# One increment per run of matmuls: no-dependency groups with a fence in a graph layer with quantile aggregation

## The chip, the cores and the metric

The kernel runs on one core of one Trainium2 chip. The metric is the device time of one execution in microseconds (us). Before the change three runs gave 2081.84, 2082.70 and 2082.77 us, so the median is 2082.7 us.

A core has five engines with a queue of instructions each: PE (TensorE, matrix products, results go to PSUM), DVE (VectorE), ACT (ScalarE), POOL (GpSimd) and SP (SyncE, here it only issues DMAs). Each works through its queue in order. They wait for each other through semaphores: an instruction can add to its engine's semaphore when it is done, and an instruction of another engine can wait until that semaphore has reached a value.

## The reference

There are 16 graphs of 1024 nodes with 64 channels each. What is computed, cut to what matters:

```python
h = max(layernorm(x), 0)
neigh = (adj > 0) & ~eye
rank = cumsum(neigh) - neigh                      # place of a neighbour in its row
nb = neigh.sum(-1)
skip = where(nb > 10, (nb + 1) // 2, 1)
rem = neigh & (skip > 1) & (rank % skip == skip - 1) & mask
rem = rem | rem.T                                 # edges that are dropped
nd = where(rem, 0, adj with ones on the diagonal) > 0
s = sort of h over the nodes of nd, for each node and channel
agg = 0.25 * q(0.25) + 0.5 * q(0.5) + 0.25 * q(0.75)   # interpolated quantiles of s
out = h + agg
y = relu(out @ W1 + b1) @ W2 + b2
return x + y * mask
```

A graph row has about eight neighbours, so the kernel keeps lists of neighbours and not matrices of values.

## The kernel before

The kernel has two ways through: `list_layer`, which runs, and `dense_layer`, a loop for inputs whose rows have too many neighbours, which the program skips here. All that follows is `list_layer`.

For each graph `b` these steps are made, as Python generators whose yields hand over to the next one:

- `load`: SP reads eight adjacency tiles of 128 x 1024 (L570), two ahead. ACT makes signs of a tile (L646), PE transposes it with eight matmuls against an identity into two PSUM tiles "tp" (L652; L657 takes the diagonal away), ACT or DVE copies them as fp8 into "ne" (L660, L662).
- `number`: 16 matmuls (L682) and eight (L689) count neighbours; six short DVE instructions (L693 to L699) follow.
- `drop`: for each half tile five matmuls (L712, L717) give the place of every neighbour in "rk", ACT takes a distance (L721), and DVE compares (L722) into "rem".
- `keep`: for each half tile six matmuls (L733, L734, L737) take dropped edges away in "kp", ACT copies (L738), then eight matmuls (L741) code the kept edges into "code", and ACT copies into "pack" (L744).
- `order`: DVE counts (L750 on), 16 matmuls (L764, L766, L770) give each node its place by number of neighbours, and DVE writes the permutation (L779).
- `collect`: for each of eight tiles nine matmuls (L801, L805) permute "pack" into "codeP", ACT copies three parts out (L809, L813, L814), and DVE draws neighbour numbers out of the codes (L819 to L848) into the list "idx". L848 is the last instruction of a list.
- `normalize`: the layer norm, on ACT (L894 to L913), and two tables of rows in DRAM.

For each pair `m` of graphs, these steps follow:

- `fetch` puts 134 gathers into a Python queue. `issue` takes them out: each is an indirect DMA on POOL (L965) and behind it a small `iota` on POOL (L942). Every fourth gather is made to wait for a DVE instruction of 12 noted instructions ago, which paces the gathers.
- `aggregate`: `sort` runs a network of minima and maxima on DVE over the gathered rows (L1000, L1003, L1007) with small pauses (L982), multiplies them by weights (L1014), and PE sums each group of rows into "acc" (L1016, L1053). `terms` splits the sum (L1028, L1030).
- `mlp`: DVE writes a 0/1 matrix "at_p" (L1077), PE brings the sums back to the order of the nodes with eight matmuls into "high" (L1096) and eight into "low" (L1099), ACT copies both (L1104, L1106), PE multiplies by W1 (L1109, L1110), ACT does the relu (L1112), and `output` multiplies by W2 (L1122, L1126) and adds x on DVE (L1129, L1130).
- Nodes with many neighbours are put together over eight graphs: `fetch_group` (L1148, L1152), `aggregate_group` and `scatter` (L1191).

PSUM has eight buffers: three of tag "mx" (tp, cp, rk, kp), one "misc" (mp, nb, ps, hp, yp and others), two "code" (code, codeP), two "agg" (acc, high, low, gacc).

`weave` mixes the results of one pair with the preparation of the graphs after the next one by costs that the generators yield. This sets the order in which instructions are written. The order in which an engine's queue holds them is made afterwards by the scheduler of the recording layer, which knows the dependencies of instructions through the tiles that they read and write and a model of times. The layer then writes the semaphores: which instruction adds to its engine's semaphore, and who waits for which value. A matmul of 7858 that `list_layer` makes stands in the queue behind a load of its weights, except where the product is of fp32.

The functions that the diff touches, and what calls them:

Of the kernel before, what the change touches and what calls it, by code (L numbers as in the profile page):

```python
# [41 lines left out]
P = 128  # L42
# [3 lines left out]
NT = N // P  # L46
# [493 lines left out]
def list_layer(  # L540
# [20 lines left out]
    psum = ctx.enter_context(tc.tile_pool(name="psum", bufs=1, space=bass.MemoryType.PSUM))  # L561
    dram = ctx.enter_context(tc.tile_pool(name="dram", bufs=2, space=bass.MemoryType.DRAM))

    asked = {}

    def ask(b, t):
# [70 lines left out]
    def load(b, fast=False):  # L637

        ne = wk.tile([P, NT, N], FP8, name="ne", bufs=2)
        neT[b] = ne  # L640
        nbs[b] = [wk.tile([P, NT], F32, name=n) for n in ("bias", "half")]
        for t in range(NT):
            ask(b, t)
            at = asked.pop((b, t))
            sg = wk.tile([P, N], BF16, name="sg")
            nc.scalar.activation(sg, at, AF.Sign)  # L646
            ask(*divmod(b * NT + t + 2, NT))
            for n in range(2):
                tp = psum.tile([P, 4, P], F32, name="tp", tag="mx", bufs=3)
                for s in range(4):  # L650
                    m = 4 * n + s
                    nc.tensor.matmul(  # L652
                        tp[:, s], sg[:, m * P:(m + 1) * P], ident16, start=(s == 0), stop=(s == 3 and t // 4 != n),
                        skip_group_check=True,
                    )
                if t // 4 == n:
                    nc.tensor.matmul(tp[:, t % 4], minus16, ident16, start=False, stop=True, skip_group_check=True)  # L657
                to = ne[:, 4 * n:4 * n + 4, t * P:(t + 1) * P]
                if fast:
                    nc.vector.tensor_scalar(to, tp, 0.0, None, OP.max, saturate=False)  # L660
                else:
                    nc.scalar.activation(to, tp, AF.Relu, saturate=False)  # L662
            if fast and t == 3:
                number(b, 0, 4)
            yield 0.1
        if fast:
            number(b, 4, NT)
        else:
            number(b, 0, NT)
        yield 1.4  # L670

    def number(b, lo, hi):
# [3 lines left out]
        for n in range(lo // 4, hi // 4):  # L676
            cols = slice(n * HALF, (n + 1) * HALF)

            cp = psum.tile([P, HALF], F32, name="cp", tag="mx", bufs=3)
            for k in range(2):  # L680
                for q in range(4):
                    nc.tensor.matmul(  # L682
                        cp[32 * q:32 * q + 32], one[:, 1 - k:33 - k], ne[:, 2 * q + k, cols], start=(k == 0),
                        stop=(k == 1), skip_group_check=True,
                    )
            nc.scalar.copy(cnt[:, cols], cp)
        nb = psum.tile([P, NT], F32, name="nb", tag="misc")
        for t in range(lo, hi):
            nc.tensor.matmul(nb[:, t:t + 1], cnt[:, t * P:(t + 1) * P], ones16[:, 0:1], start=True, stop=True)  # L689
        nb = nb[:, lo:hi]  # L690

        sk = wk.tile([P, NT], I32, name="sk")[:, lo:hi]
# [8 lines left out]
    def drop(b):  # L701

        ne = neT[b]
        bias, half = nbs[b]
        rem = wk.tile([P, NT, N], BF16, name="rem", tag="wide", bufs=1)
        rems[b] = rem
        for t in range(NT):
            ts = slice(t * P, (t + 1) * P)
            dist = wk.tile([P, N], F16, name="dist")
            for n in range(2):  # L710
                rk = psum.tile([P, HALF], F32, name="rk", tag="mx", bufs=3)
                nc.tensor.matmul(  # L712
                    rk, cnt[:, ts], blocks[:, 4 * n:4 * n + 4, None].to_broadcast([P, 4, P]), start=True, stop=False,
                    skip_group_check=True,
                )
                for s in range(4):
                    nc.tensor.matmul(  # L717
                        rk[:, s * P:(s + 1) * P], ne[:, 4 * n + s, ts], upper, start=False, stop=(s == 3),
                        skip_group_check=True,
                    )  # L720
                nc.scalar.activation(dist[:, n * HALF:(n + 1) * HALF], rk, AF.Abs, bias=bias[:, t:t + 1])  # L721
            given.append(nc.vector.tensor_scalar(rem[:, t], dist, 1.0, half[:, t:t + 1], OP.add, OP.is_equal))  # L722
            yield 0.5

    def keep(b):

        ne, rem = neT.pop(b), rems.pop(b)
        for t in range(NT):
            ts = slice(t * P, (t + 1) * P)
            kept = wk.tile([P, NT, P], FP8, name="kept")  # L730
            for n in range(2):
                kp = psum.tile([P, 4, P], F32, name="kp", tag="mx", bufs=3)
                nc.tensor.matmul(kp, plus, ne[:, 4 * n:4 * n + 4, ts], start=True, stop=False)  # L733
                nc.tensor.matmul(kp, minus, rem[:, 4 * n:4 * n + 4, ts], start=False, stop=False)  # L734
                for s in range(4):
                    at = (4 * n + s) * P
                    nc.tensor.matmul(kp[:, s], rem[:, t, at:at + P], minus, start=False, stop=(s == 3))  # L737
                nc.scalar.activation(kept[:, 4 * n:4 * n + 4], kp, AF.Relu, saturate=False)  # L738
            code = psum.tile([P, NT, 17], F32, name="code", tag="code", bufs=2)
            for s in range(NT):  # L740
                nc.tensor.matmul(  # L741
                    code[:, s], kept[:, s], octet, start=(s == 0), stop=(s == NT - 1), skip_group_check=True
                )
            nc.scalar.copy(pack[:, t, :KEYS], code.rearrange("p s k -> p (s k)"))  # L744
            yield 0.1

    def order(b):
# [12 lines left out]
        yield 1.5  # L760

        ps = psum.tile(shape, F32, name="ps", tag="misc")
        for t in range(NT):
            nc.tensor.matmul(ps, ones16, more[:, t:t + 1].to_broadcast(shape), start=(t == 0), stop=False)  # L764
        for t in range(NT - 1):
            nc.tensor.matmul(  # L766
                ps[:, t + 1:], ones16, same[:, t:t + 1].to_broadcast([P, NT - 1 - t, CAP]),
                start=False, stop=False,
            )
        nc.tensor.matmul(ps, before16, same, start=False, stop=True)  # L770
        at = wk.tile(shape, F32, name="at_e", bufs=1)
        nc.vector.tensor_tensor(at, ps, same, OP.mult)
        place_f = wk.tile([P, NT], F32, name="place_f")
# [10 lines left out]
    def collect(b, parts=((0, NT),)):  # L784
# [12 lines left out]
        for first, last in parts:  # L797
            for k in range(first, last):
                flat = psum.tile([P, PACKED], F32, name="codeP", tag="code", bufs=2)
                code = flat[:, :KEYS].rearrange("p (s k) -> p s k", k=17)  # L800
                nc.tensor.matmul(  # L801
                    flat[:, :KEYS], ones16, base[:, :KEYS], start=True, stop=False, skip_group_check=True
                )
                for t in range(NT):
                    nc.tensor.matmul(  # L805
                        flat, perm[:, t, k * P:(k + 1) * P], pack[:, t], start=False, stop=(t == NT - 1),
                        skip_group_check=True,
                    )
                nc.scalar.copy(st[:, k], flat[:, OWN:VALUES])  # L809
                halves, bytes_ = (  # L810
                    own[:, k, b % 2].bitcast(d).rearrange("p (c k) -> p c k", c=C) for d in (BF16, U8)
# [173 lines left out]
    def sort(lines, plan, first, coef, acc, in_turn=False):  # L985
# [25 lines left out]
        for n in taken:  # L1011
            now, ends = ends[:n], ends[n:]
            v = at(now[0], now[1] - now[0] if n > 1 else 0, n).rearrange("p s (k c) -> p s k c", c=C)
            nc.vector.tensor_tensor(v, v, coef(first, n)[:, :, :, None].to_broadcast(list(v.shape)), OP.mult)  # L1014
            for s in now:
                nc.tensor.matmul(  # L1016
                    acc, ident32, lines[:, s], start=False, stop=(s == now[-1] and not ends), skip_group_check=True
                )
            first += n
            cost = 0.16 + n * size / 960  # L1020
            held = let_go(held + cost)
# [64 lines left out]
    def mlp(b, o):  # L1086
# [3 lines left out]
        for n in range(2):  # L1090
# [1 line left out]
                yield from one_hot(b, n)  # L1092
            at = placed.pop((b, n))
            high = psum.tile([P, HALF], F32, name="high", tag="agg", bufs=2)
            for t in range(NT):
                nc.tensor.matmul(high, o[:, t, 0:2 * C], at[:, t], start=(t == 0), stop=(t == NT - 1))  # L1096
            low = psum.tile([P, HALF], F32, name="low", tag="agg", bufs=2)
            for t in range(NT):
                nc.tensor.matmul(  # L1099
                    low[C * (t % 2):C * (t % 2) + C], o[:, t, 2 * C:], at[:, t], start=(t < 2), stop=(t >= NT - 2),  # L1100
                    skip_group_check=True,
                )
            highs = wk.tile([P, HALF], F32, name="highs", bufs=1)
            nc.scalar.copy(highs, high)  # L1104
            lows = wk.tile([P, HALF], F32, name="lows", bufs=1)
            nc.scalar.copy(lows, low)  # L1106
            yield 1.0
            hp = psum.tile([P, HALF], F32, name="hp", tag="misc")
            nc.tensor.matmul(hp, w1, highs, start=True, stop=False)  # L1109
            nc.tensor.matmul(hp, w1, lows, start=False, stop=True)  # L1110
            h1 = wk.tile([P, HALF], F32, name="h1", bufs=1)
            nc.scalar.activation(h1, hp, AF.Relu, bias=b1c)  # L1112
            yield 1.0
# [5 lines left out]
    def output(h1, n, mask, x):  # L1119

        yp = psum.tile([P, n, C], F32, name="yp", tag="misc")
        nc.tensor.matmul(  # L1122
            yp, ones_r, b2r[:, None, :].to_broadcast([P, n, C]), start=True, stop=False, skip_group_check=True
        )
        for k in range(n):
            nc.tensor.matmul(  # L1126
                yp[:, k], h1[:, k * P:(k + 1) * P], w2, start=False, stop=(k == n - 1), skip_group_check=True
            )
        nc.vector.tensor_tensor(yp, yp, mask[:, :, None].to_broadcast([P, n, C]), OP.mult)  # L1129
        nc.vector.tensor_tensor(x, x, yp, OP.add)  # L1130

# [327 lines left out]
```

## Time and profile before

The profile is of one execution. Its span, from the first to the last instruction, is 2466.9 us; the page gives no other time of that execution. The timed runs, with a median of 2082.7 us, are of executions without a profile.

| | before |
|---|---|
| timed runs, us | 2081.84, 2082.70, 2082.77 |
| span of the profiled execution, us | 2466.9 |
| mean granted TensorE clock | 0.710 |
| gathers L965 | 1072, 1102.8 us busy, 1029 ns mean |
| sort step L1003 | 408, 280.6 us busy, 704 ns mean |
| transposing matmul L652 | 1024, 116.2 us busy, 260 ns mean |
| codeP matmul L805 | 1024, 198.3 us busy, 340 ns mean |
| sum matmul L1016 | 448 records, 160.3 us busy, 514 ns mean |
| moved by DMA | 130.22 MB, mean 53 GB/s |

How to read what the profile has: "busy" is the time in which an engine had an instruction of a row under way. A row of the waits reads: engine and line that waited, the line that released it, then the microseconds in total, how many times, and the longest. A row of the timeline reads: start, length, engine, line, operation, tiles, count, and in square brackets the idle time of the engine before it and what ended it. "issue" means that nothing the profile shows was waited for. "PEld" is the load of weights.

### The profile page before, as it was taken

To read this page: it belongs to the slowest core of one execution; us is meant where nothing else is said; L and a number is where in the kernel's file an instruction comes from. 1 tells how busy PE (TensorE), PEld (TensorE's weight loads), DVE (VectorE), ACT (ScalarE), POOL (GpSimd) and SP (SyncE) were. 2 spreads that over 40 slices of the span, in tenths; PEclk is the share of its full clock that TensorE was granted. 3 is DMA by queue.
4 is the path that set the end of the run, shared out by engine and by line. 5 is a ranking of instruction groups with operands and counts; after the bars stand their busy time and mean duration, and the time that the engine had idled before them with its cause. 6 is when DMAs were issued, how large, how long until landed. Compare 5 with 4: busy or idle time off the path is not lost.

```text
span 2466.9 us, 26583 instructions
## 1 busy us (share of the span) xinstructions
PE 1195.3 (48%) x8366; PEld 725.7 (29%) x8385; DVE 1173.0 (48%) x3635; ACT 926.8 (38%) x2414; POOL 1430.4 (58%) x2201
## 2 busy tenths in 40 slices
PE   6327165435484438345385546535565455430216
PEld 4114033222242224223153324323333233210113
DVE  3303168221356444354257452858447354931883
ACT  7428255334463236234274445433534232100001
POOL 0750846464758674676748674756577666888000
PEclk9658577667686768666686777767676777665658
DMA  3322222121313131221223131310312100111000
GB/s 109 97 64 75 62 57 73 35 60 43 91 46 77 31 89 46 48 62 41 67 71 91 42 79 29 90 46 16 93 40 60 32 17 16 42 23 20 17 0 12
DMA packets 152602, 130.22 MB, mean 53 GB/s; under 512 B 117570, under 2 KB 118082, under 8 KB 152450
## 3 DMA queue, kind: packets, MB, share of 16 engines
q1 hardware_dynamic: 116482, 91.51, 13.2%
q0 software_dynamic: 35968, 36.90, 8.4%
q8 instruction: 68, 1.11, 0.2%
q14 instruction: 84, 0.69, 0.1%
HBM read 112.78 MB, written 13.81 MB: 51 GB/s over the span
## 4 chain that ended last, share of the span: by engine, by line
PE 28%; another core or an unknown queue 22%; DVE 14%; POOL 12%; ACT 11%; issue 11%; DMA 2%; SPq 0%; POOLq 0%; DVEq 0%; ACTq 0%
POOL g L965 8%; PE codeP L805 3%; PE kp L737 3%; PE acc L1016 3%; ACT dist L721 3%; DVE g L1003 3%; DVE g L1007 2%; POOL spent L942 2%; PE kp L734 2%; PE kp L733 2%; ACT sg L646 2%; PE tp L652 2%; ACT kept L738 2%; PE rk L712 2%
## 5 line engine op out<-in xcount | busy, mean ns | idle before, releaser
L965 POOL DMA_INDIRECT g<-htab,idx x1072 | 1102.8, 1029 | 790.6 <-issue 237.6
L1003 DVE TENSOR_TENSOR g<-g 128x768 f32<-128x768 f32 (+3 forms) x408 | 280.6, 704 | 223.0 <-DMA g<-htab,idx 200.6
L942 POOL IOTA spent<- 128x128 int16 x1072 | 267.3, 249 | 44.6 <-remote 1.5
L1007 DVE TENSOR_TENSOR g<-g 128x512 f32<-128x512 f32 (+3 forms) x408 | 278.9, 702 | 22.9 <-PE acc L1053 8.4
L1016 PE MATMUL acc<-g,kf 128*128 128x256 f32 (+2 forms) x448 | 160.3, 514 | 186.2 <-DVE g L1014 160.5
L652 PE MATMUL tp<-kb,sg 128*128 128x128 bf16 x1024 | 116.2, 260 | 271.0 <-ACT sg L646 119.0
L721 ACT ACTIVATE dist<-rk,bias 128x512 f16<-128x512 f32 x256 | 172.0, 696 | 186.8 <-remote 90.2
L738 ACT ACTIVATE kept<-kp 128x512 fp8e4<-128x512 f32 x256 | 150.5, 600 | 192.0 <-remote 130.4
L662 ACT ACTIVATE ne<-tp 128x512 fp8e4<-128x512 f32 x240 | 137.3, 605 | 193.5 <-remote 136.1
L805 PE MATMUL codeP<-pack,perm 128*128 128x332 bf16 x1024 | 198.3, 340 | 9.2 <-DVE pause L982 5.5
L652 PEld LDWEIGHTS <-sg 128*128 128x128 bf16 x1024 | 88.0, 118 | 296.1 <-issue 144.5
L712 PE MATMUL rk<-kb,cnt 128*128 128x512 bf16 x256 | 118.7, 464 | 109.0 <-ACT dist L721 49.1
L722 DVE TENSOR_SCALAR rem<-dist,half 128x1024 bf16<-128x1024 f16 x128 | 64.0, 502 | 223.3 <-ACT dist L721 181.3
L741 PE MATMUL code<-kw,kept 128*128 128x17 fp8e5 x1024 | 67.8, 176 | 209.5 <-issue 99.6
L1016 PEld LDWEIGHTS acc<-g,kf 128*128 128x128 f32 x448 | 101.9, 268 | 221.9 <-DVE g L1014 170.2
L750 DVE TENSOR_REDUCE num<-pack 128x8 f32<-128x64 bf16 x16 | 4.3, 268 | 303.1 <-ACT pack L744 303.1
L717 PEld LDWEIGHTS <-ne 128*128 128x128 fp8e4 x1024 | 95.0, 114 | 165.7 <-issue 147.0
L646 ACT ACTIVATE sg<-at 128x1024 bf16<-128x1024 f32 x128 | 133.7, 1062 | 14.0 <-DMA at<-in_adj_dram 12.5
L734 PE MATMUL kp<-rem,kw 128*128 128x512 bf16 x256 | 113.8, 445 | 38.6 <-DVE g L1003 38.6
L741 PEld LDWEIGHTS <-kept 128*128 128x128 fp8e4 x1024 | 52.4, 102 | 260.8 <-issue 128.2
L805 PEld LDWEIGHTS <-perm 128*128 128x128 bf16 x1024 | 100.3, 107 | 91.3 <-issue 17.6
L737 PE MATMUL kp<-kw,rem 128*128 128x128 fp8e5 x1024 | 124.0, 244 | 0.0
(157 smaller groups left out, 2297.8 us busy)
## 6 DMA issues: line engine op xcount, KB each, us to landing
at<-in_adj_dram SPq DMA_DIRECT2D x128, 512.0 KB
g<-htab,idx POOLq DMA_INDIRECT x1072
xt<-in_x_dram SPq DMA_DIRECT2D x16, 256.0 KB
htab<-xt SPq DMA_DIRECT2D x16, 256.0 KB
gtab<-xt SPq DMA_DIRECT2D x16, 256.0 KB
y<-in_x_dram SPq DMA_DIRECT2D x16, 256.0 KB
out_dram<-y SPq DMA_DIRECT2D x16, 256.0 KB
gg<-g SPq DMA_DIRECT2D x16, 96.0 KB
```

What stands on the lines that cost most here:

```text
L646: nc.scalar.activation(sg, at, AF.Sign)
L652: nc.tensor.matmul(tp[:, s], sg[:, m * P:(m + 1) * P], ident16, start=(s == 0), stop=(s == 3 and t // 4 != n), skip_group_check=True,)
L712: nc.tensor.matmul(rk, cnt[:, ts], blocks[:, 4 * n:4 * n + 4, None].to_broadcast([P, 4, P]), start=True, stop=False, skip_group_check=True,)
L721: nc.scalar.activation(dist[:, n * HALF:(n + 1) * HALF], rk, AF.Abs, bias=bias[:, t:t + 1])
L737: nc.tensor.matmul(kp[:, s], rem[:, t, at:at + P], minus, start=False, stop=(s == 3))
L738: nc.scalar.activation(kept[:, 4 * n:4 * n + 4], kp, AF.Relu, saturate=False)
L805: nc.tensor.matmul(flat, perm[:, t, k * P:(k + 1) * P], pack[:, t], start=False, stop=(t == NT - 1), skip_group_check=True,)
L942: tc.keep_in_program_order(nc.gpsimd.iota(spent, pattern=[[1, 128]], base=0, channel_multiplier=0))
L965: return nc.gpsimd.indirect_dma_start(out=gathered[m, tiles][:, slot, k - lo, h], out_offset=None, in_=tables[2 * m + h], in_offset=bass.I ...
L1003: given.append(nc.vector.tensor_tensor(at(f, df, n), pa, pb, one))
L1007: nc.vector.tensor_tensor(pa if back else pb, pa, pb, other)
L1016: nc.tensor.matmul(acc, ident32, lines[:, s], start=False, stop=(s == now[-1] and not ends), skip_group_check=True)
```

## The change

A helper `settle` is added. It gets a list of matmuls that fill one PSUM tile, in their order. It ties each to the next by a dependency without a semaphore, puts all but the last in a group in which the layer looks for no dependencies, marks them so that they do not count on PE's semaphore, and names the last as the group's fence. Every place that fills a PSUM tile with more than one matmul collects the instructions and calls it. The matmuls, their operands and flags are the same; so are all other instructions.

```diff
+    runs = [0]
+
+    def settle(run):
+
+        runs[0] += 1
+        for ins, then in zip(run, run[1:]):
+            tc.add_manual_dep(
+                then.ins, ins.ins.name,
+                mybir.DependencyInfo(mybir.DependencyClass.NoSync, mybir.DependencyReason.DATA),
+                reason="order of a run",
+            )
+            tc.add_to_no_dep_group(f"run{runs[0]}", ins.ins)
+            tc.info.no_tile_sem_insts.add(ins.ins.name)
+        if len(run) > 1:
+            tc.declare_fence(run[-1].ins, group=f"run{runs[0]}")
...
                 tp = psum.tile([P, 4, P], F32, name="tp", tag="mx", bufs=3)
+                run = []
                 for s in range(4):
                     m = 4 * n + s
-                    nc.tensor.matmul(
+                    run.append(nc.tensor.matmul(
                         tp[:, s], sg[:, m * P:(m + 1) * P], ident16, start=(s == 0), stop=(s == 3 and t // 4 != n),
                         skip_group_check=True,
+                    ))
+                if t // 4 == n:
+                    run.append(
+                        nc.tensor.matmul(tp[:, t % 4], minus16, ident16, start=False, stop=True, skip_group_check=True)
                     )
-                if t // 4 == n:
-                    nc.tensor.matmul(tp[:, t % 4], minus16, ident16, start=False, stop=True, skip_group_check=True)
+                settle(run)
...
-            for s in now:
+            settle([
                 nc.tensor.matmul(
                     acc, ident32, lines[:, s], start=False, stop=(s == now[-1] and not ends), skip_group_check=True
                 )
+                for s in now
+            ])
...
             high = psum.tile([P, HALF], F32, name="high", tag="agg", bufs=2)
-            for t in range(NT):
+            settle([
                 nc.tensor.matmul(high, o[:, t, 0:2 * C], at[:, t], start=(t == 0), stop=(t == NT - 1))
+                for t in range(NT)
+            ])
```

The same is done to the runs of "cp" (8 matmuls), "nb" (4 or 8), "rk" (5), "kp" (6), "code" (8), "ps" (16), "codeP" (9), "low" (8), "hp" (2) and "yp" (5, or 3 for a group of nodes with many neighbours). In `sort` a run is not the whole of "acc" but the two or more rows that are summed after one multiplication. The single matmuls of "terms" and those that start "acc" are left as they were.

## The prediction

> **What bounds the kernel now.** I read the page from the top: busy shares, chain, waits, then the order of GpSimd's gathers in time.
>
> ```profile
> span 2466.9 us, 26583 instructions
> PE 1195.3 (48%) x8366; PEld 725.7 (29%) x8385; DVE 1173.0 (48%) x3635; ACT 926.8 (38%) x2414; POOL 1430.4 (58%) x2201
> PE 28%; another core or an unknown queue 22%; DVE 14%; POOL 12%; ACT 11%; issue 11%; DMA 2%; SPq 0%; POOLq 0%; DVEq 0%; ACTq 0%
> ```
>
> No engine is full; the chain of work that ended last passes through all of them. So the bound is a relay: PE, ACT and DVE make the neighbour lists, POOL gathers by them, DVE sorts, PE sums. The profiled span is 384 us longer than the median run (2466.9 against 2082.7), and the chain puts 22% down to releasers that it cannot name. I therefore use this profile for durations and differences in microseconds, which I add both to the span and to the median of 2082.7, and not for absolute shares.
>
> The waits, longest first, show the hand-overs:
>
> ```profile
> POOL g L965 <- DVE idx L848: 206.7, 6, 80.5
> DVE g L1003 <- DMA g<-htab,idx: 200.6, 24, 50.0
> POOL g L965 <- DVE pause L982: 159.6, 11, 31.8
> ACT highs L1104 <- PE high L1096: 95.7, 14, 68.2
> PE high L1096 <- DVE at_p L1077: 64.0, 3, 63.3
> ```
>
> POOL waits for the lists (L848), DVE waits for gathered rows, and 11 times POOL's wait for DVE is put down to the pause (L982), a neighbour of the awaited instruction. In POOL's timeline the two largest stalls, 70.89 and 80.53 us, lie before 250 us; after 483 us none is over 32:
>
> ```profile
> 72.78 1.10 POOL L965 DMA_INDIRECT g<-htab,idx  x1 [70.89 <-DVE idx L848]
> 247.10 0.94 POOL L965 DMA_INDIRECT g<-htab,idx  x1 [80.53 <-DVE idx L848]
> 1997.05 1.32 POOL L965 DMA_INDIRECT g<-htab,idx  x1 [11.86 <-DVE bit L844]
> 2041.07 0.95 POOL L965 DMA_INDIRECT g<-htab,idx  x1 [7.62 <-PE acc L1016]
> 2042.32 0.95 POOL L965 DMA_INDIRECT g<-htab,idx  x1 [0.30 <-issue]
> 2043.57 0.94 POOL L965 DMA_INDIRECT g<-htab,idx  x1 [0.30 <-issue]
> ```
>
> Gathers follow each other every 1.25 us (2042.32 to 2043.57), so 1072 of them are a stream of 1340 us that PE cannot shorten. Between 690 and 2270 us I count 20 stalls of POOL over 5 us, together 273 us: what a better or worse order of the other engines can move lies there.
>
> **What the Trainium skill says.** "TensorE: Matmul & The Clock Gate", section "The cost: per-tile semaphore tail": increments that matmuls make on completion serialize, about 26.3 ns each, and one increment on the last suffices because matmuls end in order. No row here shows the 26.3 ns. "Perfetto Trace Analysis", section "Tensor Engine Instruction (MATMUL, LD_WEIGHTS)": the end of a matmul in a profile is estimated, and the semaphore moves later, when PSUM has acknowledged. So a change in that tail would appear as a changed wait of ACT or DVE, not as a shorter matmul; the rows agree at least in that the 128x128 matmul is near one value (L652: 216 minimum, 219 ns median).
>
> **The change, part by part.**
>
> 1. Increments removed. The words of the change suggest 7858 matmuls that now count only at the end of each run. I built both programs and counted, in the part that runs: 1363 of 7858 matmuls carry an increment before, 1287 after. The build before already folds a run's counts into one addition (values of 5, 9 or 13) on the matmul that somebody waits for. Nobody waits for 88 of the 1363 (25 of L1096, 22 of L1016, 22 of L1109, 19 others); after, for 9. So 76 increments go, at 26.3 ns: 2.0 us if all lay on the path, 0.6 us with PE's 28% of the chain. As no row shows the price, I take 1.0 us and keep 0 to 2.0. A larger number in one addition instead of a one could have a price too; the signals that matter are the same ones, and I take nothing.
>
> 2. Waits. Of ACT's 1143 waits on PE before, 1133 name the very same matmul after; of DVE's 269, 261; of POOL's 25, all. No reader is made to wait for a later matmul in numbers that matter. PE's waits on itself go from 495 to 498. Such a wait costs at most the length of the matmul in front, 0.30 us for a codeP matmul (eight in 2.42 us on PE's timeline): 0.9 us at most. I take 0. Of these, L801's 27 waits for an older codeP tile partly pass to the first matmul of L805: one weight load later, nothing.
>
> 3. The chain of NoSync edges inside a run adds no wait: PE runs in its order anyhow. Runs do not become compact either: the output tile changes 2063 times along PE's order before and 2076 times after. No instruction, DMA or byte is added.
>
> 4. What does change is the order, since the scheduler sees other dependencies. The place differs for 4813 of PE's 15189 instructions (first at place 5364, mean shift 3.8 places over all), 1861 of DVE's 3477, 914 of ACT's, 805 of POOL's, 116 of SP's. The first third (to about 690 us of the span, counting matmuls by windows) and the last sort of the tail are untouched, and the shifts return to nearly zero in every pair of graphs.
>
> I price the order where POOL is fed. One place on DVE is 0.323 us of work (1173.0 over 3635), or 0.68 us with its idle time. The last list instruction (L848) of the graphs 6 to 15 moves on DVE by +2, +5, 0, -1, 0, -4, -1, +15, +3 and -16 places. Signed: +3 places, 1.0 us. Late ones alone: 25 places, 8.1 us (17 us at 0.68). Early ones alone: 22 places, 7.1 us (15 us at 0.68).
> The 54 sort steps that wait for a gather in both programs shift both ways as well: 11 of them five or more places earlier, 15 five or more later. A step taken earlier than its gather holds all of DVE behind it, lists included; one taken later costs nothing if the gather was late anyway. The single large move on PE is covered: one run of "high" and "low" (L1096, L1099) ends 390 places later, about 28 us of matmul work at 0.143 us each, but its reader on ACT stood behind the whole keep stage before and still does (place 1574 before, 1580 after), so the 28 us lie beside other work. If that cover failed, ACT would stand at L1104 with the next drop and codeP copies behind it, and PE behind those; the row above shows up to 68.2 us for one such wait.
> SP's 329 DMAs move by one place in the mean, and adjacency loads are asked for two tiles ahead; POOL's output writes (L1191) come three or four places earlier beside gathers of 1.25 us. Both at nothing, with 1.25 us per place if the queue were short of time.
>
> Sum. I count late lists fully and early ones not at all: a late list stops a POOL that has nothing else queued, while an early one meets a POOL still busy with the previous graph. So +8.1 - 1.0 = +7.1 us: the span would go from 2466.9 to about 2474, and the median from 2082.7 to 2089.8, say 2090.
>
> **The rivals.**
> - No change that can be told: the signed shifts count, +1.0 us, against 1.0 us of increments: 2083. For it: same waits, same first third, POOL's stream the same. This is also the case that the change does not do what it says, since the build had removed the increments already. Against it: a third of PE's and half of DVE's instructions stand elsewhere, in a relay where 20 hand-overs cost POOL 273 us.
> - Faster: the early list of graph 15 (16 places) sets when the last gathers start, and from 2041 us on POOL has hardly a gap, so the tail would move with it. Early lists and all increments: -7.1 - 2.0 = -9 us, 2074; with idle time counted, -17 us, 2066. It decides if POOL reaches the last lists with an empty queue; the page shows only 5.5 us of waiting there, which speaks against the full sum.
> - Clearly slower: one new stall of the kind seen at L1096 (63.3 us for one wait on L1077), or of a sort step taken before its gather (up to 50.0 us), in a place where POOL's queue is empty. At a third of such a length, 20 us: 2103.
>
> **How the numbers follow.** About 0.2% (4 us) is what a measurement of this kernel can tell from no change. Slightly slower, 2087 to 2098, around 2090: 0.36. Clearly slower, to 2110: 0.09. No change that can be told: 0.32. Faster: 0.23. Hence faster 0.23, same 0.32, slower 0.45. The range from 2069 to 2107 leaves out the last part of the fast case and of the clearly slower one, less than 2 in 10; the likeliest case alone has 2087 to 2098.
>
> **What would show it.** Right: busy times per engine equal within a few us, matmul rows unchanged (L652 260, L805 340 ns mean), no new wait of ACT on L1096 beyond the 95.7 us shown, and differences only in who waits for whom after 690 us. If the increments mattered, ACT's waits on PE (L809, L738, L721) would shrink in the first third too, where the order is the same. The sum is wrong if the list of graph 13 comes no later beside POOL's gathers, or if POOL's stalls between 690 and 2270 us change by tens of us.

## The result, and the profile after

The kernel after took 2094.78 us in the median of 4 runs (2093.74 to 2097.07), beside 2082.27 us for the kernel before (4 runs, 2079.16 to 2082.77). The ratio is 1.0067, with a 95% interval of 1.0053 to 1.0081: 12.5 us slower.

The profile of before that the prediction reads (span 2466.9 us) and the runs of e10, e11 and e12 below are of executions in which the kernel before took 16 to 18% longer (2422 and 2452 us beside e10 to e12), for a reason that is not known, so that they are compared among themselves alone, and the views of before below are from a second profile of the same kernel (e1, span 2071.9 us).

The page of that second profile of before, top and chain:

```profile
span 2071.9 us, 26602 instructions
...
POOL 32%; DVE 21%; PE 20%; issue 13%; ACT 9%; DMA 5%; POOLq 0%; SPq 0%; DVEq 0%; ACTq 0%
```

The same lines of the kernel after:

```profile
span 2091.9 us, 26585 instructions
PE 1099.3 (53%) x8385; PEld 684.5 (33%) x8385; DVE 1168.1 (56%) x3635; ACT 905.4 (43%) x2414; POOL 1424.3 (68%) x2201
POOL 30%; PE 23%; DVE 22%; issue 13%; ACT 8%; DMA 4%; POOLq 0%; SPq 0%; DVEq 0%; ACTq 0%
```

POOL is the largest part of both chains. Busy times say nothing of the 12.5 us: PE was busy for 1097.7 us in e1 and 1099.3 after, DVE 1168.7 and 1168.1, POOL 1425.8 and 1424.3. The waits that the prediction listed, in the kernel after (L999 is L965 of before, L882 is L848, L1037 is L1003, L1016 is L982, L1144 and L1132 are L1104 and L1096, L1113 is L1077, L769 is L741):

```profile
DVE g L1037 <- DMA g<-htab,idx: 489.0, 27, 72.3
POOL g L999 <- DVE idx L882: 133.7, 5, 70.1
ACT highs L1144 <- PE high L1132: 106.8, 21, 65.5
PE high L1132 <- DVE at_p L1113: 79.8, 9, 61.5
POOL g L999 <- DVE pause L1016: 17.1, 7, 10.3
POOL g L999 <- PE code L769: 16.1, 1, 16.1
```

POOL's waits of e1:

```profile
POOL g L965 <- issue: 236.9, 982, 1.1
POOL out_dram L1191 <- DMA out_dram<-y: 178.0, 1, 178.0
POOL g L965 <- DVE idx L848: 130.2, 4, 68.9
...
POOL g L965 <- DVE pause L982: 6.2, 11, 2.2
POOL g L965 <- DVE at_p L1077: 5.8, 2, 4.2
```

Read the last two rows of the first fence against the second: before, no single wait of a gather for the "pause" is longer than 2.2 us, after, one is 10.3; and a wait of 16.1 us appears that has no counterpart. In POOL's timeline of the kernel after these are the two stalls over 3 us between 690 us and the last gather:

```profile
1390.04 0.95 POOL L999 DMA_INDIRECT g<-htab,idx  x1 [10.30 <-DVE pause L1016]
...
1650.68 0.95 POOL L999 DMA_INDIRECT g<-htab,idx  x1 [16.12 <-PE code L769]
```

In e1 that stretch has one, of 4.2 us. All else of this document is about these two rows: whether they are the cause, and which part of the change makes them.

A correction of names: graph 0 has two L848 instructions, so that what the prediction and the expectations call the list of graph 13 is, counted from 0, that of graph 12. It is "the late list" below.

### The profile page after: what moved, and what is told of

Same layout as the page of the kernel before. It is cut to its first block, busy times and chain, and to the rows that moved or that the text cites. A ratio compares the mean times of both kernels' runs of the same rounds, so it can differ in the third digit from the quotient of the medians.

```text
span 2091.9 us, 26585 instructions
## 1 busy us (share of the span) xinstructions
PE 1099.3 (53%) x8385; PEld 684.5 (33%) x8385; DVE 1168.1 (56%) x3635; ACT 905.4 (43%) x2414; POOL 1424.3 (68%) x2201
## 4 chain that ended last, share of the span: by engine, by line
POOL 30%; PE 23%; DVE 22%; issue 13%; ACT 8%; DMA 4%; POOLq 0%; SPq 0%; DVEq 0%; ACTq 0%
POOL g L999 22%; POOL spent L976 5%; DVE g L1041 5%; DVE g L1037 5%; PE codeP L838 4%; DMA g<-htab,idx 3%; POOL gg L1191 2%; PE acc L1050 2%; PE high L1132 2%; ACT dist L746 2%; PE kp L759 2%; PE kp L760 2%; PE kp L764 2%; DVE gg L1037 2%; DVE gg L1041 2%
## 5 line engine op out<-in xcount | busy, mean ns | idle before, releaser
L999 POOL DMA_INDIRECT g<-htab,idx x1072 | 1102.4, 1028 | 430.1 <-issue 234.2
L1037 DVE TENSOR_TENSOR g<-g 128x256 f32<-128x256 f32 (+3 forms) x408 | 279.5, 702 | 543.1 <-DMA g<-htab,idx 489.0
L1050 PE MATMUL acc<-g,kf 128*128 128x256 f32 (+2 forms) x448 | 149.7, 485 | 303.7 <-DVE g L1048 278.9
L746 ACT ACTIVATE dist<-rk,bias 128x512 f16<-128x512 f32 x256 | 169.8, 702 | 175.5 <-PE rk L741 71.9
L1050 PEld LDWEIGHTS acc<-g,kf 128*128 128x128 f32 x448 | 94.3, 250 | 336.7 <-DVE g L1048 290.8
L838 PE MATMUL codeP<-pack,perm 128*128 128x332 bf16 x1024 | 189.6, 331 | 6.9 <-DVE pause L1016 5.0
L736 PE MATMUL rk<-kb,cnt 128*128 128x512 bf16 x256 | 110.3, 431 | 100.9 <-ACT dist L746 93.5
L741 PEld LDWEIGHTS <-ne 128*128 128x128 fp8e4 x1024 | 88.4, 108 | 129.5 <-issue 105.7
L760 PE MATMUL kp<-rem,kw 128*128 128x512 bf16 x256 | 100.1, 392 | 51.6 <-DVE rem L747 47.7
L1132 PE MATMUL high<-at_p,o 128*128 128x512 bf16 x256 | 75.5, 406 | 79.9 <-DVE at_p L1113 79.8
L1064 ACT CAST o<-acc 128x512 bf16<-128x512 f32 x48 | 28.2, 589 | 203.2 <-PE acc L1050 197.5
L741 PE MATMUL rk<-kw,ne 128*128 128x128 fp8e5 x1024 | 113.8, 238 | 0.0
L764 PEld LDWEIGHTS <-rem 128*128 128x128 bf16 x1024 | 80.0, 99 | 96.0 <-issue 57.1
```

The costliest lines, as they stand in the source:

```text
L741: run.append(nc.tensor.matmul(rk[:, s * P:(s + 1) * P], ne[:, 4 * n + s, ts], upper, start=False, stop=(s == 3), skip_group_check=True,))
L838: run.append(nc.tensor.matmul(flat, perm[:, t, k * P:(k + 1) * P], pack[:, t], start=False, stop=(t == NT - 1), skip_group_check=True,))
L999: return nc.gpsimd.indirect_dma_start(out=gathered[m, tiles][:, slot, k - lo, h], out_offset=None, in_=tables[2 * m + h], in_offset=bass.I ...
L1037: given.append(nc.vector.tensor_tensor(at(f, df, n), pa, pb, one))
L1050: nc.tensor.matmul(acc, ident32, lines[:, s], start=False, stop=(s == now[-1] and not ends), skip_group_check=True)
```

## The experiments

The theory, A: the change costs nothing and gains nothing by its groups, edges and unmarked increments; it makes the scheduler order the queues differently, and two instructions of the new order stop POOL. Rivals: the groups or the increments cost or gain time by themselves; or (B) the thousands of small shifts add up, and the stalls only show it.

**e1: before once more.** The kernel before, unchanged.

> The kernel before, unchanged, to get a second profile of it. The changed kernel's profile has a span of 2091.9 us, close to its timed runs, while the first profile of before had 2466.9 us, 384 us above its own. If recording stretched the first one, a second one shows about 2080 us, and the waits that it puts down to unknown releasers (22% of its chain) are gone. If the span is 2467 us again, recording costs this program more than the changed one.

Measured: 2073.63 us in one run, with a span of 2071.9. It lies below all 19 runs of the same kernel beside it (2076.72 to 2087.57 us, median 2082.04). It gives the profile of before used above; and it shows how little the span of one profile is worth for a difference of 12 us, as e3 below has the same order and a span of 2083.8. The releasers that the first profile could not name are gone from the chain. That recording stretched the first profile, as the expectation supposes, is not shown: each profiled execution from here on is one of the timed ones, about 2 us longer than its span, and e10 to e12 are long as well.

**e2: the order alone.** The kernel before, without any group, with the queues of all five engines held to the order of the kernel after:

```diff
+def follow(tc):
+    made = {i.name: i for i in tc._region_blocks()[-1].instructions}
...
+        for (step,) in struct.iter_unpack("<h", raw):
...
+                tc.add_manual_dep(
+                    made[name], before,
+                    mybir.DependencyInfo(mybir.DependencyClass.NoSync, mybir.DependencyReason.DATA),
+                    reason="given order",
+                )
```

> The kernel before without any group or fence: every matmul is tracked as before (1370 of 7858 matmuls carry an increment), but each engine's queue is given the order of the changed kernel by edges that add no wait. Theory 1, the order alone costs the time: 2095 us, ratio 1.0067, equal to the changed kernel. Theory 2, the groups themselves cost it (the size of the increments, the place of the waits): 2082 us, ratio 1.000. A mixture lies between.

Measured: 2092.10 us (6 runs, 2091.23 to 2095.94), ratio 1.0047 (1.0033 to 1.0061): 9.8 us of 2082. The kernel after has 1.0067. The intervals of the two overlap, so the order may be all of the loss, but a rest of a few us that isn't order is not ruled out.

**e3: the groups alone.** The kernel after, with its groups, edges, marks and fences, held by the same function to the order of the kernel before.

> The changed kernel with its groups and fences (1289 of 7858 matmuls carry an increment), but each engine's queue is given the order of the kernel before. Theory 1, the order alone costs the time: 2082 us, ratio 1.000 within 0.2%. Theory 2, the groups cost it: 2095 us, ratio 1.0067. My own price for the increments that are saved, 0 to 2.0 us, would put it at 2080 to 2082 us.

Measured: 2082.59 us (14 runs), ratio 1.000 (0.9989 to 1.001), with 1289 instead of 1363 matmuls that count. In this order the groups and the increments are worth nothing that these runs can tell (0.1% is 2 us); the order is the cause of the loss, as far as they can tell. The stalls go with it. POOL's waits of e2, near the first and the second:

```profile
POOL g L965 <- DVE pause L982: 10.5, 1, 10.5
```

```profile
POOL g L965 <- PE code L741: 16.1, 1, 16.1
```

In e3 no wait of a gather in these stretches (1280 to 1520 and 1640 to 1920 us) is over 1.5 us.

**Where the two stalls come from.** The first, in DVE's timeline. Before (e1):

```profile
1355.47 0.95 DVE L1014 TENSOR_TENSOR g<-g,coef 128x768 f32<-128x768 f32 x1
...
1368.10 0.56 DVE L1003 TENSOR_TENSOR g<-g 128x384 f32<-128x384 f32 x1 [11.69 <-DMA g<-htab,idx]
...
1373.16 0.36 DVE L772 TENSOR_TENSOR at_e<-ps,same 128x192 f32<-128x192 f32 x1 [1.97 <-PE ps L770]
```

After:

```profile
1374.15 1.44 DVE L1037 TENSOR_TENSOR g<-g 128x384 f32<-128x384 f32 x2 [18.80 <-DMA g<-htab,idx]
1375.63 0.96 DVE L1041 TENSOR_TENSOR g<-g 128x768 f32<-128x768 f32 x1
...
1385.94 0.95 DVE L1048 TENSOR_TENSOR g<-g,coef 128x768 f32<-128x768 f32 x1
1386.90 0.35 DVE L805 TENSOR_TENSOR at_e<-ps,same 128x192 f32<-128x192 f32 x1
...
1388.88 0.89 DVE L812 TENSOR_SCALAR perm<-iota,place_f 128x1024 bf16<-128x1024 f16 x2
```

The first sort step of one tile (128x384, "the step" below) waits for gathered rows, which land at about 1368 us in e1 and 1374 after. In the kernel before the sort and the multiplications of another tile (128x768) stand ahead of it and run while it has nothing to do; DVE is idle for 11.69 us. In the kernel after the step stands 19 places earlier, at 2190 instead of 2209: DVE is idle for 18.80 us, and the 128x768 work comes behind the wait. "at_e" starts 12.75 us after the step (1374.15 to 1386.90) and not 5.06 us (1368.10 to 1373.16); behind it come the permutation (L812), which the gather of 1390.04 waits for, and the late list. The profile puts this wait down to the pause beside the permutation; the built program names an instruction of the permutation, by which the kernel paces this gather.

The second, in PE's timeline of the kernel after:

```profile
1588.62 0.86 PE L1050 MATMUL acc<-g,kf 128*128 128x384 f32 x2
...
1633.93 0.58 PE L736 MATMUL rk<-kb,cnt 128*128 128x512 bf16 x1 [44.44 <-ACT dist L746]
...
1649.55 0.86 PE L1050 MATMUL acc<-g,kf 128*128 128x384 f32 x2
```

The gather at 1650.68 writes over a buffer that one matmul of a sum (L1050, L1016 of before) still has to read. Before, it was the second of a run of two and stood directly behind the first, at PE's places 14014 and 14015. After, the first stands at 14094 and the second at 14409 (places count matmuls and loads of weights): the edge between them keeps their order and not their neighbourhood. In between lie "drop" matmuls, ahead of which PE is idle for 44.44 us, and a whole "keep" stage. The profile puts the wait down to "code" (L769), the neighbour of the awaited matmul on PE.

**e4, e5, e6: one instruction put back.** e2's kernel, with one entry of the order moved, then the other, then both:

```diff
 PE
   I-16736   L1016 acc, first of the run
+  I-16737   L1016 acc, second of the run
 ...
-  I-16737
```

```diff
 DVE
-  I-16743   L1003, first sort step of the 128x384 tile
 ...
   I-14635   L1014, last multiplication of the 128x768 tile
+  I-16743
```

> The kernel before, without groups, with all its engines held to the order of the kernel after, except for one instruction: the second matmul of the run of two on acc_16050 (L1016, I-16737) stands again directly behind the first, instead of 315 places later. Theory A, that the 9.8 us are two stalls of POOL, each made by one misplaced instruction: the stall of 16.1 us of the gather of g1_17444 near 1660 us is gone, the one of 10.5 us near 1400 us stays, and the list of graph 13 stays 8 to 9 us late; in all 2084 to 2089 us, a ratio of 1.001 to 1.003. Theory B, that many small shifts of the order add up and the two stalls only show it: the gather then waits for another late instruction of the same stretch, and the time stays at 2091 to 2093 us, a ratio of 1.0045.

> As the run before it, but the other instruction alone is put back: the first sort step of g0_12972 (L1003, I-16743) stands 30 DVE places later, behind the last multiply of g1_11223, as it does in the kernel before; the matmul stays where the kernel after has it. Theory A: the stall of 10.5 us near 1400 us is gone, DVE's idle stretch ahead of this step falls from 19 us to about 12, and the list of graph 13 comes 8 us earlier. The stall of 16 us near 1660 us stays, and may grow, since the gathers ahead of it come earlier and the matmul does not: 2084 to 2091 us, a ratio of 1.001 to 1.004. Theory B: the list of graph 13 comes less than 3 us earlier, since the other 1860 DVE instructions of changed order are as they were; 2091 to 2093 us.

> Both instructions put back, and every other of the order of the kernel after kept. Theory A: no stall of POOL above 5 us after 690 us, and the time of the kernel before, 2080 to 2084 us, a ratio of 0.999 to 1.001: two of some 7800 instructions of changed order are the whole effect. Theory B: 2088 us or more, a ratio above 1.003, with the rest of the difference in the many small shifts.

Measured, with the other kernels for comparison. The stalls are from POOL's timelines. The interval to the late list is from the list instruction ahead of it to that of the late list. The last column is from the start of the 741st gather, ahead of both stalls, to that of the last, the 1072nd. Both are taken inside one profile each, so that what varies ahead of them doesn't count. Profiles of one order differ there too: from the 741st gather to the last, e8 has 567.8 us and e7 578.8.

| kernel | ratio (95%) | first stall, us | second stall, us | interval to the late list, us | 741st to last gather, us |
|---|---|---|---|---|---|
| before (e1) | 1 | none over 3 | none over 3 | 144.6 | 566.7 |
| e3, groups in the order before | 1.000 (0.9989 to 1.001) | none over 3 | none over 3 | 144.9 | 568.0 |
| after | 1.0067 (1.0053 to 1.0081) | 10.3 | 16.1 | 152.9 | 581.3 |
| e2, order of after | 1.0047 (1.0033 to 1.0061) | 10.5 | 16.1 | 153.1 | 581.5 |
| e4, matmul back | 1.0017 (1.0006 to 1.0028) | 10.4 | 0.5, but 9.4 nine gathers later | 152.9 | 572.8 |
| e5, step back | 1.0035 (1.0022 to 1.0049) | none over 3 | 15.7 | 143.9 | 571.5 |
| e6, both back | 1.0006 (0.9994 to 1.0018) | none over 3 | 0.5, but 7.5 nine gathers later | 144.1 | 568.0 |

The intervals to the late list can be read off one row of each trace, that of the list instruction between 1240 and 1430 us, with its first and last start. e2:

```profile
L848 DVE SCALAR_TENSOR_TENSOR idx<-bit,low x2: 257/258/259, 1261.4 to 1414.5; 128x104 int32<-128x104 f32 x2
```

e5:

```profile
L848 DVE SCALAR_TENSOR_TENSOR idx<-bit,low x2: 252/253/254, 1261.0 to 1404.9; 128x104 int32<-128x104 f32 x2
```

With both instructions back, and all other PE, DVE, ACT, POOL and SP instructions in the order of the kernel after, the time is that of the kernel before within 0.2%, and so is the stretch from the 741st gather to the last. B, which asked for a ratio above 1.003, falls: of thousands of moved instructions two make up the loss, as far as these runs can tell.

How the loss divides between the two is not settled. In ratios, putting the matmul back takes off 0.0030 (6.2 us of 2082) and the step 0.0012 (2.5 us). Worked out from the intervals of the ratios, each of these differences has about 0.002 on either side (an estimate), so that by the times alone the step's part can't be told from nothing. In the last column, from single profiles, the matmul takes off 8.7 us and the step 10.0, of 13.5 for both together. Nor is it settled why two stalls of 26.4 us together cost only 10 to 14.

One expectation was missed: in e6 a stall above 5 us remains. It is not the old one. With the matmul back, the gather that waited 16.1 us, the 926th, goes on after 0.5. Nine gathers later another one, the 935th, waits for the second matmul of another run of two of the same sum (128x128), which ends at 1648.4 us in e4. By the built programs both have moved as well: this gather was the 948th before, and the two matmuls, the 7396th and 7397th then, stand behind the 16 of "order" after, as the 7412th and 7413th. In e2 this wait does not show, presumably because the longer stall ahead of it had covered it. POOL's timeline of e4:

```profile
1627.48 0.98 POOL L965 DMA_INDIRECT g<-htab,idx  x1 [0.54 <-PE rk L717]
...
1648.69 0.94 POOL L965 DMA_INDIRECT g<-htab,idx  x1 [9.35 <-PE acc L1016]
```

The reverse, the two instructions moved in the order of before, was not tried.

**e7 and e8: which part of the change.** Built with the helper at one place alone, twelve of the thirteen places give the order of the kernel before, in all five queues. The thirteenth, "hp" (L1109 and L1110), gives the whole order of the kernel after. There the edge alone changes nothing; group and fence alone, without edge or mark, are enough. These are built programs, of which e7 and e8 were run: e7 is the kernel before with this and no more; e8 is the kernel after without it. Their traces show the same: by operation and tile, the queues of DVE, ACT, POOL and of PE's loads hold the order of the kernel after in e7 and that of e1 in e8.

```diff
 e7, against before
+            tc.add_to_no_dep_group(f"run{runs[0]}", ins.ins)
+        if len(run) > 1:
+            tc.declare_fence(run[-1].ins, group=f"run{runs[0]}")
...
-            nc.tensor.matmul(hp, w1, highs, start=True, stop=False)
-            nc.tensor.matmul(hp, w1, lows, start=False, stop=True)
+            settle([
+                nc.tensor.matmul(hp, w1, highs, start=True, stop=False),
+                nc.tensor.matmul(hp, w1, lows, start=False, stop=True),
+            ])
```

```diff
 e8, against after
-            settle([
+            list([
                 nc.tensor.matmul(hp, w1, highs, start=True, stop=False),
```

> The kernel before, with one thing of the change alone: the first of the two matmuls of hp (L1109, L1110) is put in a no-dependency group whose fence is the second, in all 34 places; no edges, no marks against counting, no other run touched. Built, all five engines' queues hold the order of the kernel after, instruction by instruction, and 1370 matmuls count. Theory A, that the group of hp reorders the program and the two misplaced instructions of that order cost the time: the two stalls of POOL near 1400 and 1660 us are there, and the time is 2090 to 2094 us, a ratio of 1.004 to 1.006. A theory in which the other twelve kinds of runs cost something of their own: 2083 to 2087 us, ratio under 1.003.

> The kernel after, with its groups, edges, marks and fences in every place but hp, whose two matmuls are left as they were before. Built, all queues hold the order of the kernel before, with no order forced by hand, and 1314 of 7858 matmuls count. Theory A: 2080 to 2084 us, a ratio of 0.999 to 1.001, no stall of POOL over 5 us after 690 us. If the groups of the other twelve kinds cost or gain something: more than 0.2% away from the kernel before, either side.

Measured: e7 2091.91 us, ratio 1.0047 (1.0029 to 1.0064), with stalls of 10.4 and 15.3 us. e8 2080.25 us (22 runs), ratio 0.9991 (0.998 to 1.0002), with no stall over 3 us after 1270 us (one of 5.7 us at 1254, the one of 4.2 us in e1). POOL's timeline of e7:

```profile
1393.39 0.95 POOL L993 DMA_INDIRECT g<-htab,idx  x1 [10.44 <-DVE pause L1010]
...
1651.93 0.94 POOL L993 DMA_INDIRECT g<-htab,idx  x1 [15.31 <-PE code L763]
```

So the loss of the change hangs on a group for one pair of matmuls, and the other twelve kinds of runs cost nothing that these runs can tell. Whether e8 gains a little (0.09%, up to 0.2% by its interval) stays open. Why the scheduler, given this group, takes two more matmuls of "high", with their loads, ahead of a "codeP" run (PE's place 5364, the first difference) was not looked into.

**e9: is POOL the bound?** If stalls of POOL cost time, a faster POOL should gain it. One size is changed, in the order before; `spent` is read by nobody.

```diff
-            tc.keep_in_program_order(nc.gpsimd.iota(spent, pattern=[[1, 128]], base=0, channel_multiplier=0))
+            tc.keep_in_program_order(nc.gpsimd.iota(spent[:, 0:8], pattern=[[1, 8]], base=0, channel_multiplier=0))
```

> The kernel before in its own order, with one size changed: the small iota behind each of the 1072 gathers writes 8 numbers a partition instead of 128. Theory A says that from about 570 to 1920 us POOL's stream of gathers is what bounds the time, so that a stall of POOL is paid nearly in full. If so, 0.1 to 0.15 us less per gather saves 60 to 120 us of 2082, unless the gaps between gathers (0.30 us) grow by as much. The rival, that the hand-overs between engines bound the time and POOL only looks full: less than 20 us saved, with longer waits of POOL for DVE and for lists.

Measured: 2009.69 us, ratio 0.9649 (0.9629 to 0.9669), 73.9 us less than the 2083.58 of before beside it. POOL's timeline of e1, and then of e9, in a stretch without stalls:

```profile
1616.26 0.94 POOL L965 DMA_INDIRECT g<-htab,idx  x1 [0.16 <-issue]
1617.21 0.25 POOL L942 IOTA spent<- 128x128 int16 x1
1617.62 0.94 POOL L965 DMA_INDIRECT g<-htab,idx  x1 [0.16 <-issue]
```

```profile
1613.15 0.94 POOL L965 DMA_INDIRECT g<-htab,idx  x1 [0.16 <-issue]
1614.11 0.15 POOL L942 IOTA spent<- 128x8 int16 x1
1614.42 0.94 POOL L965 DMA_INDIRECT g<-htab,idx  x1 [0.16 <-issue]
```

From gather to gather it is 1.36 us with the long iota and 1.27 with the short one where an iota stands between them, as behind about half of the 1072 gathers; elsewhere gathers stand in rows, 1.25 us apart where nothing delays them, and their iotas in blocks behind. Over all, the iotas' busy time falls by 107 us (264.7 to 157.6), and 73.9 of these come off the end, with DVE's instructions as long as before (950 ns for a sort step of 128x768 in both). So most of what POOL is spared comes off the time, which is why a stall of it costs anything. This version beats both kernels.

**e10, e11, e12: order and iota together.** e10 is e9's iota in the order of the kernel after. e11 and e12 are one kernel: e8 with an iota of one number, and no order given.

```diff
-            tc.keep_in_program_order(nc.gpsimd.iota(spent, pattern=[[1, 128]], base=0, channel_multiplier=0))
+            tc.keep_in_program_order(nc.gpsimd.iota(spent[:, 0:1], pattern=[[1, 1]], base=0, channel_multiplier=0))
```

> As the run with the short iota (2009.7 us), but held to the order of the kernel after. Theory A: with POOL some 0.07 us faster a gather, the two misplaced instructions, which wait for work of other engines, come no sooner, so POOL meets them with as long a stall or a longer one. The two stalls are there, and the time is 2017 to 2035 us, 8 to 25 us more than the same iota in the order before. If instead the slack of a faster POOL swallows them: 2008 to 2013 us.

> A version to keep: the kernel after with hp's two matmuls left ungrouped, and the iota behind each gather writing one number a partition. No order is forced; the scheduler, which counts the iota's time too, moves 1294 PE and 628 DVE instructions, but not the two that matter. Theory A: about the time of the short iota, 2000 to 2015 us, ratio 0.960 to 0.968. If the new order of 616 POOL instructions brings a stall of its own: 2015 to 2030 us.

> The same kernel as in the run before, on whatever chip comes. If the kernel before takes about 2082 us there, POOL is its bound and theory A gives 2000 to 2015 us, a ratio of 0.960 to 0.968; a stall made by the new order, 2015 to 2030 us. If the kernel before takes about 2420 us there, POOL is not the bound and the ratio is again 1.00 to 1.03.

Measured: e10 2454.26 us, ratio 1.016 (1.0084 to 1.0236); e11 2478.31, ratio 1.0217 (1.015 to 1.0283), both beside 2422.5 us for before; e12 2507.69 beside 2452.0, ratio 1.0252 (1.0191 to 1.0314). These do not answer what e10 and e11 asked, since POOL is not the bound in them: it has 5% of e12's chain, against 32% in e1. The ratio of e12 is in the range that its expectation gave for such a case. The first three rows of POOL's waits of e12:

```profile
POOL g L999 <- issue: 236.8, 957, 2.1
POOL g L999 <- DVE idx L882: 217.2, 5, 82.0
POOL g L999 <- DVE pause L1016: 189.7, 18, 35.8
```

These two waits for DVE make up 407 us here, against 136.4 in e1 (130.2 and 6.2) and 366.3 in the prediction's profile of before (206.7 and 159.6): POOL waits for the others, and a shorter iota bought nothing here. That the kernel of e11 gains where e9 does was not shown; nor why it lost over 2% here.

## Why the prediction was right, and where it was wrong

**The time.** 2090 was forecast, with a range of 2069 to 2107 and "slower" as the likeliest sign; 2094.8 came. In ratios to before, +7.1 us was forecast and +12.5 measured; e2 and e7, with the same order, have +9.8 (0.0047 of 2082). That the number came so near is in part luck, as the parts below show. By a sign that the prediction itself named, stalls of POOL that change by tens of us, its sum was wrong: there are 26.4 us of new stalls.

**Increments (step 1, -1.0 us).** The count was right: few go, as the build had folded them. The gain of 1.0 us isn't there: e3, with 74 fewer than before, gives 1.000 with an interval of 0.1% on either side, which also holds 1.0 us. The sign that was named, shorter waits of ACT on L809, L738 and L721 in the first third, is not clear: up to 570 us the three are 118.5 us in e1, 116.9 in e3, 118.2 in e8 and 112.0 in the kernel after. "TensorE: Matmul & The Clock Gate", section "The cost: per-tile semaphore tail", of the Trainium skill has 26.3 ns for each increment, fitted to small matmuls that are packed into the array and run at once; 76 of them at 2.0 us are below what these runs can tell, and no run here confirms or refutes the figure.

**Waits (2) and edges (3).** Right: e3 and e8 show that the waits and edges, in the order of before, cost nothing that can be told. The matmul rows hardly change, as forecast: L652 has 249 ns in e1 and 248 after, L805 324 and 331. The remark that an edge does not make a run compact was right too, and was put at nothing; it is the second stall. A run that had stood together by itself was torn, and an edge without a semaphore doesn't hold it.

**The order (4): the mechanism.** Right in kind: the loss lies after 690 us, the late list is the one that was named, and it came later by 8.0 to 8.5 us (interval 152.9 and 153.1 against 144.6 and 144.9), with a gather waiting. The price was made otherwise than the prediction made it. It multiplied 15 places by 0.323 us of work, 4.8 us of its 8.1. The 8 us are the work of another tile that had run in the shadow of a wait for a gather, and now comes after it: the sentence "A step taken earlier than its gather holds all of DVE behind it" was there, with 11 such steps counted, and was given no term of the sum. So the 8.1 us of the sum and the 8.0 to 8.5 us of this one list agree by chance.

The faster rival (2074 us) rested on the list of graph 15, by the prediction's count, 16 places earlier on DVE. It came 169.8 us behind the late list in the kernel after and in e2, and 168.1 to 168.8 us behind it in e1, e3 and e8 (167.5 in e7, which has the order of after): earlier in place is not earlier in time, since DVE waits for others in between. Nothing of that gain showed.

**The order: what was missed.** "The single large move on PE is covered" failed. The 390 places of "high" and "low" were covered: ACT waits for L1132 for 106.8 us in all and 65.5 at most after, 101.3 and 68.4 in e1. But it was not the only large move: the second matmul of the torn run stands 394 places later than before. Its stall of 16.1 us, some 6 to 9 us of the loss by e4, had no term in the sum. Moves read by groups of instructions instead of one by one hide it.

**POOL's stalls.** "20 stalls of POOL over 5 us, together 273 us" between 690 and 2270 us came from a profile whose span is 384 us longer than the timed median. In e1 there is no stall over 5 us between 690 us and the last gather (at 1873 us). The prediction saw the misfit and kept the profile's differences; it should have kept only its durations. Its stream of 1340 us also leaves out the iotas, which take 264.7 us of POOL in e1. In the timed runs the bound is less "a relay" than POOL's stream, which has 32% of the chain, the largest part, and from which a shorter iota takes 73.9 us (e9).

**The rivals.** "No change that can be told" is what e8 and e3 have, so it would have been right without "hp". "Clearly slower" by one stall of 20 us was the right kind: two, of 10.3 and 16.1 us, which are 26.4 us together and cost 9.8 to 12.5.

## What to carry to other kernels

A change of dependencies alone can be a change of order: compare the order of every engine's queue instruction by instruction, and look first at the ones that an engine with no slack waits for. Build the change one place at a time before judging it: here one pair of matmuls in thirteen places made all of the new order, and leaving it out made the change free. A wait for data is cheap as long as other work stands ahead of the waiting instruction; moved ahead of that work, it delays everything behind it by that work, here by some 8 us. And a profile whose span doesn't fit the timed runs is good for durations of instructions, not for what bounds them.

## What the runs showed of the hardware

The iota on POOL took 247 ns for 128 numbers a partition (median of 1072, e1), 147 for 8 (e9; 148 in e10) and 132 for one (e12). Between 8 and 128 numbers that is 0.83 ns for each further one (100 ns over 120), and between one and 8 it is 2.1 (15 ns over 7), so one fixed cost and one price a number do not fit all three. The starts of the gathers around an iota say the same of the first two: 1.36 us against 1.27. Two gathers with nothing between them started 1.25 us apart (e4). Leaving 74 matmuls uncounted, with the order held, had no effect that an interval of 0.1% shows (e3).
